# Layer 1's taps for the last sample: from one tap in 64x64 tiles to four taps at a time in 128x32 tiles

## The chip, the core and the metric

The kernel runs on one core of a Trainium2 chip. The core has five engines with instruction queues of their own: TensorE (PE, matrix products, with a separate row PEld for loading the stationary operand), VectorE (DVE), ScalarE (ACT), GpSimd (POOL) and SyncE (SP), which here only issues DMAs. The engines run side by side and wait for each other by semaphores; inside one engine the order is fixed. The metric is the device time of one launch in microseconds (us). Numbers are float32 throughout, and every matmul call of the program shows as two instruction records on PE.

## The reference, cut to what matters

The input is x of shape (4, 256, 48, 48): four samples, 256 channels (two halves k = 0, 1 of 128 channels), 2304 positions. Four layers are applied in turn, each as x = x + layer(groupnorm(x)): layer 0 is an attention of 8 heads, layer 1 a gate made by depthwise convolutions, layer 2 a second attention with one head, layer 3 a depthwise 3x3 convolution with normalisation. Layer 1, which the change touches, is:

```python
x_tem = _blur_pool(_max_pool_3x3(x), stride=3)            # 48x48 -> 16x16
x_h1 = _dwconv(x_tem, w_h1, ((5, 5), (1, 1)))             # 11x3 taps
x_w1 = _dwconv(x_tem, w_v1, ((1, 1), (5, 5)))             # 3x11 taps
x_h2 = _inv_h_transform(_dwconv(_h_transform(x_tem), w_h2, ((5, 5), (1, 1))))  # 11x3 along a diagonal
x_w2 = _inv_v_transform(_dwconv(_v_transform(x_tem), w_v2, ((1, 1), (5, 5))))
gate = sigmoid(batchnorm(x_h1 + x_w1 + x_h2 + x_w2))      # 16x16, then repeated 3x3
out = x * gate_upsampled
```

All four convolutions together are one depthwise convolution of a 16x16 image per channel with 81 distinct offsets (`TAPS`), whose weights are first gathered on a 13x13 grid per channel.

## The kernel before, in words

The order of all instructions is written out by the program itself. The main loop is `attend`. It goes through groups: a group is two blocks of 128 keys of one attention unit of 384 queries, and nine groups make a unit. In each group PE does the scores of this group (L309), then what is put in between (tables `fills` and `due`, and generators called lanes), then the weighted sum of the group before (L329). ScalarE takes the exponent (L315, `pt`), GpSimd adds the two blocks of a group (L340, `half`), VectorE adds these up (L355, `acc`). At the third group of the next unit the sums of the exponents are taken (`total`, L362), copied by ScalarE into two `row` tiles of the pool `op` (tag "o", two buffers), and sent through four small SP DMAs (L375); two groups later they are inverted (`invert`, L382 to L397) and spread by SP DMAs (L387, L392).

Layer 0 takes 864 groups, then layer 2 takes 27 groups for each of the four samples. We write group (s.g) for group g of 27 in the layer 2 attention of sample s. Other work rides in the groups: samples 0 to 2 have their layer 1 done during layer 0 of the sample behind them, on ScalarE and VectorE (`strips`). The last sample, b = 3, has its layer 1 done in the groups of layer 2 of samples 0 to 2, in the lanes of `l1_last`: `tops` (the maxima and the blur on VectorE, first k = 0 and then k = 1), `sums` (the 81 taps, on PE, `strips_pe`), and `gates` (the gate, the multiplication of x, the statistics for layer 2's norm). Each lane makes at most one step in a group, and none in groups 0, 9 and 18. `follow` waits for the norm's result `nb`, and two groups later starts the projections of sample 3 for its layer 2 (`start`, L1022 and L1028, and slices of L1058 and L1079). What is left of it in group (2.26) is emitted there at once, and sample 3's attention begins in (3.0).

`strips_pe` before: the blurred 16x16 image is put in the middle of a padded 28x28 tile `pd` (`padded`, memset by POOL at L856, filled by ACT at L859). A depthwise tap on PE is a product with a diagonal matrix of weights. `build` makes 12 such matrices of 64 columns on POOL (L927), `product` (L943) multiplies, with 64x64 tiles: the channels 0 to 63 and 64 to 127 apart, and the odd and the even taps apart, so that four tiles are in the array side by side. Rounds of 12 taps go to two PSUM tiles from `pj_tile` (a pool of two buffers that all the other work uses too), ScalarE copies them out in four pieces of 64x256 (L951), VectorE adds (L958, L961). There are seven rounds for each k, none of them in a group listed in `taken` (groups that already hold w_stats, a projection slice, or a `total`).

`w_stats` (L1112 on PE, L1120 on VectorE) also takes two `pj` tiles at a time and holds them until VectorE has read them. `gn` takes the group norm: `squares` (L228), `inverse` (L238, and the root on POOL, L179), `done` (L247 and L249 on VectorE, which give `nb`).

`tap_weights` prepares the tap weights once, in the first unit of layer 0: the grid, the list `wt` of 81 weights (L764), on POOL, one small piece in a group.

Of the kernel before, what the change touches and what calls it, by code (L numbers as in the profile page):

```python
# [14 lines left out]
P = 128  # L15
# [63 lines left out]
def usual_path(  # L79
# [648 lines left out]

    def tap_weights():
# [6 lines left out]
        nc.gpsimd.tensor_add(ident2, ident[:, 0:D], ident[:, D:P])  # L736
        yield 2
# [21 lines left out]
        while i < len(TAPS):  # L759
            dr, dc = TAPS[i]  # L760
            n = 1
            while i + n < len(TAPS) and TAPS[i + n] == (dr, dc + n):
                n += 1
            nc.gpsimd.tensor_copy(wt[:, :, i : i + n], g2[:, :, dr + 6, dc + 6 : dc + 6 + n])  # L764
            i += n
            yield 1
        v1 = lp.tile([P, NK], F32, name="v1")
# [6 lines left out]
    WEIGHT_TICKS = 26  # L774

    NT = 4
# [3 lines left out]
    L1_BUF = (NT + 1) * AS * AS  # L780
# [123 lines left out]
    TAPS_AT_ONCE = 12  # L904

    AT_PLACE = 7

    def strips_pe(b, k, norm, res):


        rounds = [
            range(i, min(i + TAPS_AT_ONCE, len(TAPS)))
            for i in range(0, len(TAPS), TAPS_AT_ONCE)
        ]
        diag = {}
        acc = lp.tile([P, AS, AS], F32, tag=("l1acc", "blur2")[k], name="l1acc")
        res["acc"] = acc
        parts = wo.rearrange("p c n -> p (c n)").rearrange(
            "p (i h r c) -> p i h r c", i=2, h=2, c=AS
        )  # L920

        def build(n):
            taps = rounds[n]
            xs = xsp.tile([P, NK, SL + 1], F32, tag="xs", name="diag1")
            xs = xs.rearrange("p k s -> p (k s)")[:, : len(taps) * D]
            diag[n] = xs.rearrange("p (t j) -> p t j", j=D)
            nc.gpsimd.tensor_tensor(  # L927
                diag[n], ident2.unsqueeze(1).to_broadcast([P, len(taps), D]),
                wt[:, k, taps[0] : taps[-1] + 1].unsqueeze(2).to_broadcast([P, len(taps), D]),
                ALU.mult,  # L930
            )

        def product(n):
            taps = rounds[n]
            ps = [pj_tile()[:, : AS * AS] for _ in HALVES]
            runs = [taps[0::2], taps[1::2]]
            for i in range(len(runs[0])):
                for h, r in enumerate(HALVES):
                    for e, run in enumerate(runs):
                        if i >= len(run):  # L940
                            continue
                        dr, dc = TAPS[run[i]]
                        nc.tensor.matmul(  # L943
                            ps[h][HALVES[h ^ e]].rearrange("p (r c) -> p r c", c=AS),
                            lhsT=diag[n][r, run[i] - taps[0], :],
                            rhs=pd[r, PAD + dr : PAD + dr + AS, PAD + dc : PAD + dc + AS],
                            start=i == 0, stop=i == len(run) - 1,
                        )
            for h, r in enumerate(HALVES):
                for e in range(2):  # L950
                    nc.scalar.copy(  # L951
                        parts[r, n % 2, e].rearrange("p r c -> p (r c)"), ps[h][HALVES[h ^ e]]
                    )

        def add(n):
            two = parts[:, n % 2]
            if n == 0:
                nc.vector.tensor_add(acc, two[:, 0], two[:, 1])  # L958
                return
            for e in range(2):  # L960
                nc.vector.tensor_add(acc, acc, two[:, e])  # L961
# [3 lines left out]
        while "blurred" not in res or "nb" not in norm:  # L965
            yield 1
        pd = padded(k, norm, res)
        res["padded"] = True
        yield 1
        for n in range(len(rounds)):  # L970
            while clock["t"] in taken:
# [1905 lines left out]
```

## Time and profile before

| what | value |
|---|---|
| median of 3 runs | 3520.81 us (3519.45 to 3521.15) |
| the profiled execution | 3522.7 us |
| its span, first to last instruction | 3520.9 us |
| granted TensorE clock, mean | 0.995 |
| layer 2 of samples 0, 1, 2, 3 begins at | 2904.1, 3020.7, 3155.5, 3266.1 us |
| the taps on PE (L943), first and last start | 2985.3, 3166.7 us |
| L943 records, busy | 648, 42.8 us |

A line of a group reads: line, engine, operation, tile written <- tiles read, array tile, shape, count | busy us, mean ns of one | idle time before it and what ended it. A line of a timeline reads: start, length, engine, line, operation, and in brackets the idle time before it and what ended it. Matmul records overlap, so the pace of PE is read from the distance of starts: 16 records of L309 start 1.29 us before the next 16 of L329.

### The profile page before, as it was taken

The numbers are of one execution on the slowest core, as the hardware profiler recorded it, in microseconds if no ns is written. First come the engines' busy times: TensorE is split into PE (matmuls) and PEld (weight loads), VectorE is DVE, ScalarE is ACT, GpSimd is POOL, SyncE is SP. The second block draws the span as 40 slices with busy tenths as digits, with TensorE's granted clock in tenths as the row PEclk, the third lists the DMA queues.
The fourth block names the chain that finished last, engine by engine and source line by source line (L and its number), as shares of the span: only waits on it lengthen the run. The fifth ranks groups of instructions, "written<-read, shape, count | busy, mean of one in ns | idle before, by whom it ended". The sixth has DMA issues, their size and how long they took to land. (4 is left out here: it accounts for less than half of the span.)

```text
span 3520.9 us, 88613 instructions
## 1 busy us (share of the span) xinstructions
PE 3438.4 (98%) x37158; PEld 1740.7 (49%) x37158; DVE 2559.1 (73%) x3456; ACT 2386.1 (68%) x3855; POOL 796.8 (23%) x666
## 2 busy tenths in 40 slices
PE   9999999999999999999999999999999999999988
PEld 5554555554444444444444444444444444555533
DVE  3555545467888788687887886878887878657777
ACT  5665666665886796557866976679668755555576
POOL 2333333321111000011110110101010106567432
PEclk9999999999999999999999999999999999999999
DMA  2211111111111111121111111111111110000067
GB/s 89 49 26 22 26 22 26 22 26 22 22 32 22 27 22 26 43 57 21 26 22 27 22 26 18 26 22 26 19 25 15 29 13 4 6 6 8 4 150 226
DMA packets 121897, 116.63 MB, mean 33 GB/s; under 512 B 58848, under 2 KB 112976, under 8 KB 120720
## 3 DMA queue, kind: packets, MB, share of 16 engines
q1 hardware_dynamic: 120240, 108.97, 16.4%
q8 instruction: 293, 4.80, 0.6%
q10 hardware_dynamic: 1248, 1.91, 0.2%
q14 instruction: 116, 0.95, 0.1%
HBM read 56.99 MB, written 11.80 MB: 20 GB/s over the span
## 5 line engine op out<-in xcount | busy, mean ns | idle before, releaser
L315 ACT ACTIVATE pt<-sc 128x768 f32<-128x768 f32 x1944 | 1474.8, 811 | 729.6 <-PE sc L309 722.0
L355 DVE TENSOR_TENSOR acc<-acc,pt 128x768 f32<-128x768 f32 x1368 | 1368.1, 1000 | 171.6 <-ACT pt L315 72.1
L329 PE MATMUL av<-pt,v 64*64 64x384 f32 x13824 | 1274.8, 484 | 0.0
L309 PE MATMUL sc<-q,k 64*64 64x384 f32 x13824 | 1270.0, 482 | 0.5 <-ACT pt L315 0.5
L309 PEld LDWEIGHTS sc<-q,k 64*64 64x64 f32 x13824 | 525.5, 133 | 589.4 <-issue 542.7
L329 PEld LDWEIGHTS av<-pt,v 64*64 64x64 f32 x13824 | 518.2, 133 | 599.1 <-issue 565.7
L410 POOL TENSOR_TENSOR o<-o,rinv 128x384 f32<-128x384 f32 x95 | 115.3, 1213 | 1731.2 <-DMA rinv<-rinv 1724.2
L340 POOL TENSOR_TENSOR half<-pt 128x768 f32<-128x768 f32 x189 | 363.0, 1924 | 532.2 <-ACT pt L315 492.5
L700 DVE SCALAR_TENSOR_TENSOR x<-pj,bo,x 128x384 f32<-128x384 f32 x192 | 118.5, 617 | 313.1 <-PE pj L687 311.7
L355 DVE TENSOR_TENSOR acc<-acc,half 128x768 f32<-128x768 f32 x171 | 192.2, 1124 | 207.4 <-POOL half L340 206.4
L876 ACT ACTIVATE prod<-pd,wt 128x256 f32<-128x256 f32 x486 | 337.3, 765 | 0.2
L604 PE MATMUL pj<-xs,w 128*128 128x384 f32 (+1 forms) x720 | 275.4, 505 | 0.0
L604 PEld LDWEIGHTS pj<-xs,w 128*128 128x128 f32 x720 | 124.1, 189 | 127.9 <-issue 38.3
L329 PE MATMUL av<-pt,qv 64*64 64x384 f32 x1728 | 174.7, 492 | 0.0
L309 PE MATMUL sc<-qv,kd 64*64 64x384 f32 x1728 | 171.6, 486 | 2.4 <-ACT pt L315 2.4
L899 DVE TENSOR_REDUCE prod<-prod 128x256 f32<-128x1280 f32 x114 | 168.7, 1480 | 0.7 <-ACT prod L876 0.7
L687 PE MATMUL pj<-o,wo 128*128 128x384 f32 (+1 forms) x384 | 160.1, 500 | 7.2 <-issue 3.6
L635 PEld LDWEIGHTS pj<-w,xs 128*128 128x128 f32 x1080 | 134.5, 191 | 24.2 <-issue 1.2
L349 DVE TENSOR_TENSOR acc<-pt 128x768 f32<-128x768 f32 x99 | 115.5, 1166 | 40.2 <-ACT pt L315 40.2
L406 POOL TENSOR_TENSOR o<-raw 128x384 f32<-128x384 f32 x95 | 128.9, 1357 | 50.5 <-ACT raw L402 50.0
L635 PE MATMUL pj<-w,xs 128*128 128x128 f32 x1080 | 134.9, 275 | 0.0
L402 ACT COPY raw<-av 128x768 f32<-128x768 f32 x108 | 86.3, 799 | 48.3 <-PE av L329 44.9
(291 smaller groups left out, 2421.2 us busy)
## 6 DMA issues: line engine op xcount, KB each, us to landing
xs<-in_x_dram SPq DMA_DIRECT2D x90, 384.0 KB
sh<-pad SPq DMA_DIRECT2D x126, 162.2 KB
rinv<-rinv SPq DMA_DIRECT2D x208, 94.5 KB
out_dram<-x SPq DMA_DIRECT2D x23, 384.0 KB
l<-row SPq DMA_DIRECT2D x416, 1.5 KB
w<-in_wqkv_dram SPq DMA_DIRECT2D x32, 192.0 KB
x<-in_x_dram SPq DMA_DIRECT2D x4, 1152.0 KB
x<-in_x_dram SPq DMA_DIRECT2D x9, 384.0 KB
```

Of the source, the lines that this page charges most:

```text
L309: nc.tensor.matmul(ps[c * D : (c + 1) * D, h, :SL], lhsT=u["of"]["k"][r, j0 : j0 + D], rhs=u["of"]["q"][r, u["qc"]], start=True, stop=True,)
L315: nc.scalar.activation(pt, ps[:, :, :SL], AF.Exp, scale=u["scale"])
L329: nc.tensor.matmul(u["av"][h * D : (h + 1) * D, half, :SL], lhsT=value(u, j, h)[r], rhs=pt[r, h, :], start=j == 0, stop=j == JB - 1,)
L340: nc.gpsimd.tensor_add(half, pts[0], pts[1])
L355: nc.vector.tensor_add(u["acc"], u["acc"], term)
L406: eng.tensor_add(u["sum"], u["raw"][:, 0, :], u["raw"][:, 1, :])
L604: nc.tensor.matmul(ps[:, :n], lhsT=at["w"][:, k, t, :], rhs=xs[s][:, k, :n], start=k == 0, stop=k == NK - 1,)
L635: nc.tensor.matmul(ps[:, i * P : (i + 1) * P], lhsT=xs[s][:, k, i * P : (i + 1) * P], rhs=at["w"][:, k, 2, :], start=k == 0, stop=k == NK - 1,
L687: nc.tensor.matmul(ps[:, :n], lhsT=wo[:, p, k * P : (k + 1) * P], rhs=o["o"][:, :n], start=True, stop=True,)
L700: nc.vector.scalar_tensor_tensor(xs, ps[:, :SL], pair["bo"][:, k : k + 1], xs, ALU.add, ALU.add)
L876: nc.scalar.activation(bufs[n % 3][:, :, min(n, 1) + i].rearrange("p (r c) -> p r c", c=AS), pd[:, PAD + dr : PAD + dr + AS, PAD + dc : PA ...
L899: nc.vector.tensor_reduce(to, bufs[n % 3][:, :, : min(n, 1) + len(taps)], AX.X, ALU.add)
```

## The change

The 81 offsets become sums over stacks. A stack is a set of four buffers, one for each block of 32 channels, whose four blocks of 32 partitions hold the same 32 channels of `pd`, shifted by 0, 1, 2 and 3 times a step. One matmul with 128 rows and 32 columns then applies four taps to 32 channels, and the four blocks j of 32 channels go to the four column tiles side by side. Four stacks per k (`STACKS`) with 9, 6, 3 and 3 products cover the taps: 21 products of 4 taps instead of 81 single ones. `place` fills a stack with 16 SP DMAs from SBUF to SBUF, each of 32 partitions with 465 to 634 float32; the buffers are tiles that are free at that time: the last attention output buffer `Y[1]` ("y"), `t1` and `t2` ("t", from the maxima), `t3` and `wo` ("w").

Both k go through one lane: eight stacks in the order `ORDER3`, ten rounds. Eight DMAs are issued in a step; a stack's product comes at the earliest three steps (`SETTLED`) after its last DMA was issued; a buffer set is filled again only after the products that read it have been emitted. A round now takes one PSUM tile, one ScalarE copy of 128x256 and, except for each k's first, one VectorE addition; the copy goes to a tile of tag "o" of the pool `op`. `gates` for a k starts when that k's last round was added.

`tap_weights` gets more work in the first unit of layer 0: 27 small POOL copies and a memset into `rolled`, a small POOL addition, and 16 SP DMAs of 32 partitions into `stacked`, the weights in the order in which the products read them.

```diff
@@ tap_weights
+        nc.gpsimd.tensor_add(ident2[:, 0:32], ident2[:, 0:32], ident2[:, 32:64])
...
+        rolled = lp.tile([P, L1_BUF], F32, tag="t3", name="rolled")
+        nc.gpsimd.memset(rolled[:, 0, :, 6:9], 0.0)
+        for q in range(4):
+            parts = [
...
+            for to, fr in parts:
+                nc.gpsimd.tensor_copy(to, fr)
+            yield 1
+        for q in range(4):
+            for j in range(4):
+                nc.sync.dma_start(
+                    stacked[32 * q : 32 * q + 32, j], rolled[32 * j : 32 * j + 32, q]
+                )
+            yield 1
...
-    WEIGHT_TICKS = 26
+    WEIGHT_TICKS = 34
...
+    STACKS = [
+        (PW + 5, PW, 634, [PW * a + c for a in (0, 4, 7) for c in range(3)]),
+        (5 * PW + 1, 1, 499, [PW * r + c for r in range(3) for c in (0, 7)]),
+        (8 * PW + 3, PW - 1, 465, [0, 1, PW + 1]),
+        (11, PW - 1, 465, [PW, PW + 1, 0]),
+    ]
+    ROUNDS3 = (((0, 6), (6, 9)), ((9, 15),), ((15, 18),), ((18, 21),))
+    ORDER3 = [
+        (0, 1, "y"), (0, 2, "y"), (0, 3, "y"), (0, 0, "t"), (1, 1, "w"), (1, 0, "t"), (1, 2, "w"),
+        (1, 3, "t"),
+    ]
+    FILLS_AT_ONCE = 8
+    SETTLED = 3
@@ strips_pe
         def build(n):
+            _, k, _, (m0, m1) = rounds[n]
...
+            shape = [P, m1 - m0, 4, 32]
             nc.gpsimd.tensor_tensor(
-                diag[n], ident2.unsqueeze(1).to_broadcast([P, len(taps), D]),
-                wt[:, k, taps[0] : taps[-1] + 1].unsqueeze(2).to_broadcast([P, len(taps), D]),
-                ALU.mult,
+                diag[n], ident2[:, 0:32].unsqueeze(1).unsqueeze(1).to_broadcast(shape),
+                stacked[:, :, k, m0:m1].rearrange("p j m -> p m j").unsqueeze(3)
+                .to_broadcast(shape), ALU.mult,
+            )
+        def place(u, n):
...
+            q, j = divmod(n, 4)
+            c0 = (j % 2) * size
+            nc.sync.dma_start(
+                bufs[u][j // 2][32 * q : 32 * q + 32, c0 : c0 + size],
+                pd[k][32 * j : 32 * j + 32, start + step * q : start + step * q + size],
             )
         def product(n):
-            ps = [pj_tile()[:, : AS * AS] for _ in HALVES]
...
+            ps = pj_tile()[:, : AS * AS]
+            for m in range(m0, m1):
+                for j in range(4):
+                    c0 = (j % 2) * size + offsets[m - FIRST3[i]]
+                    rhs = bufs[u][j // 2][:, c0 : c0 + AS * PW]
+                    nc.tensor.matmul(
+                        ps[32 * j : 32 * j + 32].rearrange("p (r c) -> p r c", c=AS),
+                        lhsT=diag[n][:, m - m0, j, :],
+                        rhs=rhs.rearrange("p (r c) -> p r c", c=PW)[:, :, 0:AS],
+                        start=m == m0, stop=m == m1 - 1,
                     )
-            for h, r in enumerate(HALVES):
-                for e in range(2):
-                    nc.scalar.copy(
-                        parts[r, n % 2, e].rearrange("p r c -> p (r c)"), ps[h][HALVES[h ^ e]]
+            if n == first[k]:
+                part[n] = None
+                nc.scalar.copy(acc[k], ps)
+            else:
+                part[n] = op.tile([P, SL + 1], F32, tag="o", name="part")[:, : AS * AS]
+                nc.scalar.copy(part[n], ps)
...
+        def may_fill(u, n):
+            k, _, which = ORDER3[u]
+            before = [v for v in range(u) if ORDER3[v][2] == which]
+            if before and n <= max(m for m, r in enumerate(rounds) if r[0] == before[-1]):
+                return False
+            if which != "y" and "blurred" not in res[1]:
+                return False
+            if k not in pd:
+                if "blurred" not in res[k] or "nb" not in norm:
+                    return False
+                pd[k] = padded(k, norm, res[k]).rearrange("p r c -> p (r c)")
+                res[k]["padded"] = True
+                return False
+            return True
 
         build(0)
         build(1)
+        left = [(u, c) for u in range(len(ORDER3)) for c in range(16)]
+        n, placed, seen = 0, {}, 0
+        while n < len(rounds):
+            add()
+            u = rounds[n][0]
+            if u in placed and seen >= placed[u] + SETTLED and clock["t"] not in taken:
+                product(n)
+                n += 1
+                if n + 1 < len(rounds):
+                    build(n + 1)
+            for _ in range(FILLS_AT_ONCE):
+                if not left or not may_fill(left[0][0], n):
+                    break
+                v, c = left.pop(0)
+                place(v, c)
+                if c == 15:
+                    placed[v] = seen
+            seen += 1
             yield 1
```

## The prediction

> **What bounds the kernel now.** I read the page's busy shares first, then the groups of PE in layer 2 (2904 to 3266 us), the busy times by stretch, the timeline of PE around the taps, and last the DMA issues of SP.
>
> ```profile
> PE 3438.4 (98%) x37158; PEld 1740.7 (49%) x37158; DVE 2559.1 (73%) x3456; ACT 2386.1 (68%) x3855; POOL 796.8 (23%) x666
> ```
>
> PE is the bound over the whole span. Whether it is so in the changed stretch is told by the stretches there (length; then busy PE, PEld, DVE, ACT, POOL; clock):
>
> ```profile
> 2985.00:3060.00 75.00, 67.99 (x832) 43.43 (x833) 59.24 (x69) 38.72 (x70) 46.60 (x25) 0.95 0.08 7
> 3060.00:3155.00 95.00, 88.70 (x1038) 56.11 (x1040) 47.20 (x62) 52.50 (x92) 57.94 (x33) 0.98 0.06 6
> 3155.00:3245.00 90.00, 84.34 (x1033) 49.57 (x1025) 72.47 (x88) 49.40 (x76) 70.30 (x38) 0.98 0.10 8
> ```
>
> PE is at 91 to 94%, so it leads, but VectorE is at 79% and 81% in the first and third stretch, and the clock dips below 1. The groups say how much of PE is taps, and that 128x32-like tiles already run in layer 3 (96*32):
>
> ```profile
> L943 PE MATMUL pj<-pd,diag 64*64 64x256 f32 x648 | 42.8, 399 | 9.8 <-DVE bst L1120 6.7 <-ACT pd L859 3.1
> ```
>
> ```profile
> L309 PE MATMUL sc<-q,k 64*64 64x384 f32 x13824 | 1270.0, 482 | 0.5 <-ACT pt L315 0.5
> ...
> L1730 PE MATMUL cv<-sh,taps 96*32 96x384 f32 (+1 forms) x1152 | 104.5, 503 | 1.8 <-DMA sh<-pad 1.1 <-ACT junk L1593 0.7
> ```
>
> Busy time over records is 91.9 ns for L309 and 90.7 ns for L1730: a record of 32-column tiles costs what a record of 64x64 tiles costs, four being in the array at once in both. The timeline gives the pace and the stalls:
>
> ```profile
> 2931.18 1.47 PE L309 MATMUL sc<-qv,kd 64*64 64x384 f32 x16
> 2932.58 2.85 PE L1058 MATMUL pj<-x,w 128*128 128x384 f32 x8
> ...
> 2985.32 2.93 PE L943 MATMUL pj<-pd,diag 64*64 64x256 f32 x48 [3.06 <-ACT pd L859]
> ...
> 3016.76 2.88 PE L943 MATMUL pj<-pd,diag 64*64 64x256 f32 x48
> 3019.41 1.52 PE L329 MATMUL av<-pt,qv 64*64 64x384 f32 x16
> ...
> 3050.89 5.44 PE L943 MATMUL pj<-pd,diag 64*64 64x256 f32 x48 [4.07 <-DVE bst L1120]
> ...
> 3085.18 1.63 PE L309 MATMUL sc<-qv,kd 64*64 64x384 f32 x16 [2.41 <-ACT pt L315]
> ...
> 3205.63 1.37 PE L1112 MATMUL pj<-y,Ww 64*64 64x384 f32 x5 [4.08 <-DVE bst L1120]
> ```
>
> An undisturbed round of 48 records takes 3019.41 - 3016.76 = 2.65 us of PE, 55.2 ns a record. Around the rounds PE stands still where VectorE is late with `bst`, and where ScalarE waits for `pd`.
>
> **PE's stream: -17.2 us.** Before: 81 taps x 2 halves of channels x 2 k = 324 calls, 648 records, x 55.2 ns = 35.8 us. After: 21 products x 4 blocks x 2 k = 168 calls, 336 records of the same 256 columns, 18.6 us.
>
> **Switching the array's tiles: +2.2 us.** The old rounds were 64x64 between 64x64 neighbours; the new ones switch to 128x32 and back, 10 rounds x 2. The row: L309's 16 records cost 1.29 us, yet L1058, in 128*128, starts 1.40 us after them, so a switch costs 0.11 us and 20 cost 2.2. The Trainium skill ("TensorEngine Tiling (Array Packing)", Tiling Modes, Key Properties) speaks against the change: a change of tiling mode drains the array. It gives no time; if a drain costs the constant of an isolated matmul, 398 cycles at 2.4 GHz = 0.166 us ("TensorE: Matmul & The Clock Gate", Single matmul latency), 20 make 3.3 us as an estimate and the sum is 1.1 us worse. I take the row.
>
> **ScalarE, VectorE and POOL per round: nothing by themselves.**
>
> ```profile
> L927 POOL TENSOR_TENSOR diag<-ident,wt 128x768 f32<-128x768 f32 (+1 forms) x14 | 29.1, 2082 | 31.8 <-PE pj L943 31.8
> L951 ACT COPY wo<-pj 64x256 f32<-64x256 f32 x56 | 20.5, 366 | 33.6 <-PE pj L943 32.7
> L961 DVE TENSOR_TENSOR l1acc<-l1acc,wo 128x256 f32<-128x256 f32 x24 | 16.3, 677 | 11.1 <-ACT wo L951 9.9
> ```
>
> ScalarE goes from 56 to 10 copies (20.5 to about 4 us; the copy of twice the partitions has the same 256 columns), VectorE from 26 additions to 8 (18.7 to 5.4 us), POOL from 10368 to 5376 elements in `build` (29.1 to 15 us). ScalarE's gain hides behind PE; VectorE's shows only through its stalls, next.
>
> **Stalls of PE that were there.** (a) 3.06 us for `pd` at group (0.20): POOL's memset only ended at 2984.6 and ScalarE, held by `pd`, can't take the next exponent either. With the round gone, PE meets the same wait at the scores of (0.21) instead. -0.4. (b) 4.07 us at (1.6), and the round then took 5.44 us instead of 2.65: 6.9 us in all. In (0.20) to (1.6) PE loses 13.3 us of old rounds (five, 2.65 each) against 4 us of new ones; VectorE loses 6.3 us of additions (L958, L961) and some of POOL's interference. PE comes some 11 us earlier, VectorE, which waited 6.2 us for POOL at 3023 when POOL stood behind a `build` that waited for a round, comes perhaps 10 earlier. Between 0 and -6.9; I take half, -3.5. (c) 2.41 us at (1.13) for the second `pd`, when two builds of 3.6 us stood before the memset on POOL; they no longer do. But the memset now waits until 16 fills have read the old `pd`. Between 0 and -4, I take -2. (d) 4.08 us at (2.14): the gate's work on VectorE moves, see below; 0, between -2 and +3.
>
> The clock: after 4.07 us of standing the 48 records took 2.8 us too long, after 3.06 us nothing was lost (2.93). The skill ("TensorE: Matmul & The Clock Gate", Part 1) says that an idle window of about 3.4 us halves the clock, in agreement; by it any new wait over that length costs about 2 us more, by the rows of this trace waits up to 3 us cost only themselves. My new waits stay below.
>
> **The fills: +2.5 us.**
>
> ```profile
> L1607 SPq DMA_DIRECT2D sh<-pad x126: 507/588/1824, 3364.4 to 3486.4; - x126
> ```
>
> ```profile
> 2992.22 2.43 SPq L375 DMA_DIRECT2D l<-row  x4
> ```
>
> 128 fills at 0.588 us are 75 us of SP, 9.4 us a stack, and SP is otherwise almost empty here (10 issues a unit). What they move, 8.4 MB (16 x 32 rows x 634, 499, 465, 465 float32, twice), is light: layer 3 moved 202 GB/s. By the code's rules the steps come out so: `pd` in (0.19), fills (0.20, 0.21), rounds at (0.24), (1.2), (1.6), (1.15), (1.19), (1.20), (1.24), (1.26), (2.1), (2.6). The same counting reproduces where the old rounds stand in the trace. At (0.24): eight fills run from 2985.3 to 2990, the four `l` DMAs of (0.21) come next and end near 2992.5, the other eight end near 2997 and have landed by 2999, while PE gets there near 2997: 2 us of waiting. At (1.6) the margin is about zero, elsewhere three groups or more remain. Queued behind the fills are `l` and `rinv`; in (1.19) to (1.23) SP falls 10 us behind, but `rinv` of that unit is wanted only four groups and a projection slice later (about 20 us). Between 0 and +8.
>
> **Two "o" buffers: +1.5 us.** Round (1.2) writes a `part`, its addition is emitted in (1.3) behind `total`, whose second `row` needs the same buffer. So ScalarE's row copy waits until VectorE is through the maxima of that step (L831, L832: 3.7 us in the trace), with the next exponent behind it. Between 0 and +4.
>
> **The end of the chain: +3 us, and +1.** The last old round is at (2.2), the gate at (2.4), `nb` at (2.23), `start` at (2.25). The new last round is at (2.6), the gate at (2.7), `squares` at (2.22), `inverse` at (2.24), `nb` and `start` both at (2.26), the last group. There PE waits: the root on POOL comes after VectorE's L240, so `half` of (2.24), which ended at 3242.3, ends near 3244.9, its `acc` near 3246, `nb` near 3247, and PE would be there at 3243.9. 3 us, between 0 and 7. `squares` and `inverse` also need `pj` tiles next to w_stats in (2.22): +1.
>
> **Weights in layer 0: 0.** 27 copies (17 such took 5.4 us), and 16 DMAs (9.4 us), in a stage where POOL is busy 13 to 20 us of 40 and waits for ScalarE. Without that cover some 9 us of POOL would show.
>
> **Sum:** -17.2 + 2.2 - 0.4 - 3.5 - 2 + 2.5 + 1.5 + 3 + 1 = -12.9 us. The profiled execution of 3522.7 us (1.8 us of it outside the span) becomes 3509.8. The median lies 1.9 us under that execution, so 3507.9 us.
>
> **Rivals.** *VectorE sets the pace* in the first and third stretch: stalls (b) and (c) keep their length (+5.5 against my sum), the additions of (1.3) cost 4 (+2.5), and the late gate crowds VectorE at (2.11) to (2.14) where w_stats waits for it (+2): -2.9, 3518 us. For it: 79 to 81% and the `bst` waits. Against it: 52 us of VectorE's idle time in layer 2 are waits for POOL, which gets lighter. *The stalls go wholly*: (b) -6.9, (c) -4, no wait for fills: -20.8, 3500 us. *Late fills, slower than before*: each product waits for its stack in PE's order, and nothing passes it. It decides from 12.9 / 8 = 1.6 us per stack beyond my sum. At 3 us per stack, +24, the kernel takes 3532 us. For it: only three short groups (7.7 us) between the last eight issues and the product, 4.7 us of issuing and the `l` DMAs between. Against it: most groups here last 3 to 6 us, and in layer 3 the first product after 16 such issues waited 1.07 us for a DMA. *That the tiles don't run four abreast* would leave a stream of 18.6 us longer; L1730 excludes it.
>
> **How the numbers follow.** My case 0.61, with a range of its own of 3503 to 3513; stalls gone 0.13; VectorE's pace 0.18; late fills 0.08. A measurement here can tell 0.2%, 7 us, from no change: above 3513.8 is "same". Faster: 0.93 of my case, all of the second, a fifth of VectorE's, 0.74 or about 0.75; slower is the last case, 0.08, and 0.17 is left for the same. The range of 8 in 10 leaves out the slow case and the best tail: 3499 to 3518.5.
>
> **What would show it.** Right: 336 records for the taps in about 21 us busy; the rounds in the groups named; the round at (1.6) without a dip of the clock; `start` in the last group of sample 2's attention behind a wait for `nb`; layer 3 and layer 0 unchanged in length. Wrong: PE's idle time before the taps released by a DMA for more than 13 us in all; or layer 2 of sample 1 as long as before in spite of fewer records, with `bst` as the releaser.

## The result, and the profile after

| | before | after |
|---|---|---|
| median (8 runs each, side by side) | 3520.97 us (3517.73 to 3523.21) | 3508.83 us (3505.00 to 3512.72) |
| ratio, with its 95% interval | 1 | 0.9965 (0.9956 to 0.9974) |
| the profiled execution; its span | 3522.7; 3520.9 us | 3510.3; 3508.6 us |
| tap records on PE, busy | 648, 42.8 us | 336, 24.8 us |

The changed kernel is 12.1 us faster; 3507.9 us was predicted. The share of busy time hardly moves, since PE leads in both:

```profile
PE 3430.5 (98%) x36846; PEld 1721.6 (49%) x36846; DVE 2543.4 (72%) x3438; ACT 2369.3 (68%) x3809; POOL 798.9 (23%) x691
```

The groups of layer 2 (line, engine, tile, shape, count | busy, mean ns | idle before, releaser) show the three kinds of buffers of the taps, and the lighter work of GpSimd, ScalarE and VectorE:

```profile
L1016 PE MATMUL pj<-stack,diag 128*32 128x256 f32 x204 | 16.8, 422 | 2.1 <-issue 2.1
...
L971 POOL TENSOR_TENSOR diag<-ident,stacked 128x384 f32<-128x384 f32 (+1 forms) x10 | 14.3, 1438 | 28.6 <-PE pj L1016 28.6
...
L1016 PE MATMUL pj<-y,diag 128*32 128x256 f32 x96 | 8.0, 437 | 4.0 <-DVE bst L1216 4.0
...
L1033 DVE TENSOR_TENSOR l1acc<-l1acc,part 128x256 f32<-128x256 f32 x8 | 6.6, 826 | 7.4 <-ACT part L1027 7.4
...
L1016 PE MATMUL pj<-wo,diag 128*32 128x256 f32 x36 | 4.4, 387 | 0.0
...
L1027 ACT COPY part<-pj 128x256 f32<-128x256 f32 x8 | 3.0, 372 | 15.2 <-PE pj L1016 10.8 <-issue 4.4
```

No idle time of PE ahead of L1016 is put down to a DMA. What PE waited for in layer 2 (us in total, times, longest):

```profile
PE pj L1016 <- DVE bst L1216: 4.0, 2, 2.1
PE pj L1208 <- DVE bst L1216: 3.6, 2, 3.5
...
PE pj L1208 <- ACT row L371: 2.5, 1, 2.5
```

The taps waited 6.7 us for `bst` and 3.1 us for `pd` before; now 4.0 us for `bst`, 2.1 us for "issue" (which the last experiment resolves), and `w_stats` waits in other places. An undisturbed round of 24 records, and three of the places where PE stands, look so on PE's timeline:

```profile
3102.89 1.47 PE L309 MATMUL sc<-qv,kd 64*64 64x384 f32 x16
3104.29 1.53 PE L1016 MATMUL pj<-stack,diag 128*32 128x256 f32 x24
3105.75 1.52 PE L329 MATMUL av<-pt,qv 64*64 64x384 f32 x16
3107.09 1.47 PE L309 MATMUL sc<-qv,kd 64*64 64x384 f32 x16
...
3193.16 2.01 PE L1208 MATMUL pj<-y,Ww 64*64 64x384 f32 x8 [3.49 <-DVE bst L1216]
...
3221.38 0.38 PE L228 MATMUL pj<-mx,gmat 128*128 128x2 f32 x2 [2.43 <-DVE bst L1216]
...
3236.18 0.61 PE L1118 MATMUL pj<-gn_nb,w2c 128*128 128x1 f32 x4 [1.13 <-DVE gn_nb L249]
```

From 3102.89 to 3104.29 are 1.40 us where L309's 16 records cost 1.29; the 24 records take 1.46 us where 24 x 55.2 ns are 1.32; the next 16 take 1.34 us instead of 1.29. So a round pays 0.11 + 0.14 + 0.05 = 0.30 us for its change of tiles.

Each unit of attention has one sum of exponents (L362 in groups (s.3), (s.12), (s.21)), which marks the same place in every kernel. The changed kernel was profiled three times in all (here, and twice below). From one L362 to the next, with the prediction's sum cut up at the same places (tap records x 55.2 ns, 0.22 us a round for tiles, and its other terms where it put them):

| from, to | before | after, three profiles | mean difference | predicted |
|---|---|---|---|---|
| (0.12), (0.21) | 37.9 | 35.0, 34.8, 34.6 | -3.1 | -3.1 |
| (0.21), (1.12) | 89.9 | 84.4, 83.0, 83.5 | -6.3 | -8.8 |
| (1.12), (1.21) | 46.7 | 40.0, 41.7, 41.7 | -5.6 | -2.7 |
| (1.21), (2.3) | 41.8 | 42.3, 40.7, 40.7 | -0.6 | -4.0 |
| (2.3), (2.12) | 25.8 | 26.8, 26.8, 26.8 | +1.0 | +1.5 |
| (2.12), (2.21) | 32.1 | 31.7, 31.7, 29.2 | -1.2 | 0 |
| (2.21), (3.3) | 48.1 | 52.4, 52.5, 54.5 | +5.0 | +4 |
| sum | 322.4 | 312.7, 311.1, 310.9 | -10.9 | -12.9 |

Before was profiled once, in an execution 1.7 us above its median; the three of the changed kernel lie 3.3 us below theirs in the mean. So a row is good to one or two us.

Outside these units no term was predicted. There the recorded execution of after lost 1.6 us between the first score of layer 2 and the first L362, and from the last one to the end took 241.4 us for 245.8 (241.1 and 240.4 in its other two profiles). Of these 4.8 us in the mean, 1.5 come from the change: up to the first L1601 of layer 3 all three profiles took 82.4 or 82.5 us, and before took 83.9 to the same place, with one more wait of 1.05 us for `bst`; the run that moves the last stack, below, brings both back. Most of the rest differs between executions: the kernel before with light rounds, below, took 242.3 us for the whole stretch.

### The profile page after: what moved, and what is told of

Same layout as the page of the kernel before. It is cut to its first block, busy times and chain, and to the rows that moved or that the text cites. A ratio compares the mean times of both kernels' runs of the same rounds, so it can differ in the third digit from the quotient of the medians.

```text
span 3508.6 us, 88105 instructions
## 1 busy us (share of the span) xinstructions
PE 3430.5 (98%) x36846; PEld 1721.6 (49%) x36846; DVE 2543.4 (72%) x3438; ACT 2369.3 (68%) x3809; POOL 798.9 (23%) x691
## 5 line engine op out<-in xcount | busy, mean ns | idle before, releaser
L355 DVE TENSOR_TENSOR acc<-acc,pt 128x768 f32<-128x768 f32 x1368 | 1369.1, 1001 | 173.6 <-ACT pt L315 74.6
L309 PE MATMUL sc<-q,k 64*64 64x384 f32 x13824 | 1270.2, 483 | 0.5 <-ACT pt L315 0.5
L309 PEld LDWEIGHTS sc<-q,k 64*64 64x64 f32 x13824 | 526.1, 133 | 588.8 <-issue 542.1
L700 DVE SCALAR_TENSOR_TENSOR x<-pj,bo,x 128x384 f32<-128x384 f32 x192 | 118.5, 617 | 312.3 <-PE pj L687 310.9
L355 DVE TENSOR_TENSOR acc<-acc,half 128x768 f32<-128x768 f32 x171 | 186.5, 1090 | 207.7 <-POOL half L340 207.0
L309 PE MATMUL sc<-qv,kd 64*64 64x384 f32 x1728 | 168.6, 492 | 1.2 <-ACT pt L315 1.1
L406 POOL TENSOR_TENSOR o<-raw 128x384 f32<-128x384 f32 x95 | 128.7, 1355 | 48.4 <-ACT raw L402 48.1
```

The lines of the kernel that those rows point to most:

```text
L309: nc.tensor.matmul(ps[c * D : (c + 1) * D, h, :SL], lhsT=u["of"]["k"][r, j0 : j0 + D], rhs=u["of"]["q"][r, u["qc"]], start=True, stop=True,)
L355: nc.vector.tensor_add(u["acc"], u["acc"], term)
L406: eng.tensor_add(u["sum"], u["raw"][:, 0, :], u["raw"][:, 1, :])
```

## The experiments

Theory: the gain is PE's shorter stream of taps, less a few waits that the new order makes. Rivals: the gain is the lighter work of the helpers; the fills limit it; VectorE has become the bound. Line numbers of the experiments are up to five higher than the changed kernel's; those of the light rounds go with the kernel before (L944 there for L943, L1108 for L1112, `bst` L1116 for L1120).

**Twice and a third of the products.** Dose for PE's stream, the helpers' work unchanged.

```diff
-                    nc.tensor.matmul(
+                    for twice in range(2):
+                        nc.tensor.matmul(
...
-                        start=m == m0, stop=m == m1 - 1,
+                            start=m == m0 and twice == 0, stop=m == m1 - 1 and twice == 1,
```

> The changed kernel with each of the 168 calls for the taps issued twice, so the sum of the taps comes out doubled; all else is as it was: the same fills, copies, additions and builds. PE's stream of taps is 672 records instead of 336, close to the 648 of the kernel before, but without its 46 extra copies and 18 extra additions. Theory (the gain is PE's stream): 336 records at 55 ns put back 18.5 us, so 3508.8 + 18.5 = about 3527 us, between 3522 and 3531, a little above the kernel before. Rival (the gain came from the lighter rounds of ScalarE, VectorE and GpSimd, and PE's records mostly fell into its waits): less than 8 us come back, below 3517 us.

```diff
+            m1 = m0 + (m1 - m0) // 3
             for m in range(m0, m1):
```

> The changed kernel with only the first third of each round's products: 112 records for the taps instead of 336, all copies, additions, builds and fills as they were (54 of the 81 taps, padded weights of zero aside, are left out of the sum). In the run with doubled products 336 more records made the stretch from the first sum of the exponents to (2.21) 15.2 us longer, 45 ns a record, and the time 16 us. Theory (PE's stream sets the pace on the way down too): 224 records fewer give 10 us, between 8 and 12.5 us below the changed kernel. Rival (with the changed kernel VectorE has become the bound of layer 2, at 79 to 81% busy and with most of PE's waits put down to bst): less than 4 us.

Doubled: 3523.45 us, 1.0012 of before (1.0006 to 1.0019). A third: 3491.17 us, 0.9923 (0.9911 to 0.9936). The L362 of (0.12) and of (2.21) on PE's timeline, first of the changed kernel, then doubled, then a third:

```profile
2954.47 0.82 PE L362 MATMUL pj<-acc,ones 64*64 64x384 f32 x8
...
3214.75 0.97 PE L362 MATMUL pj<-acc,ones 64*64 64x384 f32 x8
```

```profile
2952.25 0.82 PE L362 MATMUL pj<-acc,ones 64*64 64x384 f32 x8
...
3226.08 0.97 PE L362 MATMUL pj<-acc,ones 64*64 64x384 f32 x8
```

```profile
2949.42 0.82 PE L362 MATMUL pj<-acc,ones 64*64 64x384 f32 x8
...
3194.16 0.97 PE L362 MATMUL pj<-acc,ones 64*64 64x384 f32 x8
```

That is 260.3, 273.8 and 244.7 us; the mean of the three profiles of the changed kernel is 258.5. 336 records more cost 15.4 us there (46 ns each), 224 fewer give 13.7 us (61 ns each), around the 55 ns of the prediction; the three profiles of the changed kernel themselves lie between 256.4 and 260.3 us. Single rounds are free of that scatter. The round of 24 records above has 8 in the run with a third:

```profile
3092.55 0.65 PE L1017 MATMUL pj<-stack,diag 128*32 128x256 f32 x8
3093.13 1.52 PE L329 MATMUL av<-pt,qv 64*64 64x384 f32 x16
```

0.58 us for 1.46: 16 records are 0.88 us, 55 ns each. In the medians the gain of the third is 20 us against the changed kernel beside it; the expectation of 8 to 12.5 us was too small. Of the 6 us that these units do not show, 2 lie in the first stretch of layer 2 (46.9 us for a mean of 49.1, by the clock, see below), and most of the rest is that the profiled executions of the changed kernel were faster than its median: their mean is 3507.0 us, 17.5 above that of the third. The rival "VectorE is now the bound" would have given under 4 us: it falls. The theory's main term stands in both directions.

**The kernel before with light rounds.** One copy, one VectorE operation and half a build per round, PE's 648 records kept.

```diff
-                diag[n], ident2.unsqueeze(1).to_broadcast([P, len(taps), D]),
+                diag[n], ident2.unsqueeze(1).to_broadcast([P, half, D]),
...
-            for h, r in enumerate(HALVES):
-                for e in range(2):
-                    nc.scalar.copy(
-                        parts[r, n % 2, e].rearrange("p r c -> p (r c)"), ps[h][HALVES[h ^ e]]
-                    )
+            nc.scalar.copy(parts[:, n % 2, 0].rearrange("p r c -> p (r c)"), ps[1])
...
-            for e in range(2):
-                nc.vector.tensor_add(acc, acc, two[:, e])
+            nc.vector.tensor_add(acc, acc, two[:, 0])
```

> The kernel before with all 648 tap records on PE, but with its other engines' work per round cut to about that of the changed kernel: one copy of 128x256 on ScalarE instead of four of 64x256, one VectorE operation instead of two, builds of 6 matrices instead of 12. It leaves out the products of one PSUM tile in each round and reads wrong weights for half of the taps. Theory: PE's stream is what counts, and of the lighter rounds only stalls (b) and (c) of the prediction, 5.5 us, can go: between 0 and 5.5 us below the kernel before, 3515.5 to 3521 us. Rival (lighter rounds): most of the 12 us of the change, so 3509 to 3513 us.

Measured: 3516.92 us, 0.9990 of before (0.9982 to 0.9998), some 2 to 4 us (1 to 6 by the interval). PE's waits in layer 2:

```profile
PE pj L944 <- DVE bst L1116: 5.0, 3, 2.1
...
PE pj L1108 <- DVE bst L1116: 4.1, 1, 4.1
PE pj L944 <- ACT pd L859: 3.1, 1, 3.1
```

The taps' wait for `bst` at (1.6) goes from 4.07 to 1.81 us, while the one at (1.15) grows from 1.56 to 2.09; the other two lines keep their length. So lighter helpers alone give a quarter or so of the change, by the interval at most about half; the rival falls, and stall (b) is shown to depend on them in part. The gain stands in the medians alone: from (0.12) to (3.3) the profiled execution took 324.0 us for 322.4, with dips of the clock (0.57 from 3146 to 3152 us).

**The fills: each one twice, then each one in two halves.**

```diff
+            for _ in range(2):
                 nc.sync.dma_start(
```

> The changed kernel with every one of the 128 fill DMAs issued twice in a row, to the same place: 75 us more of SP, 9.4 us a stack, counted in the same groups. In the trace of the changed kernel no wait of PE is put down to a DMA, but the first stack's last fill landed at 3001.1 us and its product started at 3002.05 us, 1 us later. Theory (fills are hidden, with little margin at the first stack and three groups or more at the others): about 8 us at the first stack less what its wait for bst (1.9 us) covers, up to 3 us at the third one, nothing elsewhere: +6 to +11 us, 3515 to 3520 us. Rival (the fills and their queue are what the change pays with, in every stack): +3 us or more for each of eight stacks, above 3532 us. Second rival (there is slack everywhere): below 3511 us.

Measured: 3732.61 us, 1.0608 of before (1.0593 to 1.0622). Neither expectation foresaw 214 us, and the edit did more than double the issues: the second DMA writes where the first has just written and waits for it to land. SP's waits from 2900 to 3300 us:

```profile
SPq L1004 <- DMA stack<-pd: 70.2, 44, 4.3
SPq L1004 <- DMA y<-pd: 68.6, 48, 4.0
```

It measured an ordering of DMAs that the change doesn't have. So the next one cut each fill in two, with the same bytes and no place written twice:

```diff
-            nc.sync.dma_start(
-                bufs[u][j // 2][32 * q : 32 * q + 32, c0 : c0 + size],
...
+            cut = size // 2
+            for a, z in ((0, cut), (cut, size)):
+                nc.sync.dma_start(
+                    bufs[u][j // 2][32 * q : 32 * q + 32, c0 + a : c0 + z],
```

> The changed kernel with each fill cut into two DMAs of half the columns: 256 DMAs, the same bytes, 9.4 us more of SP per stack, and no DMA writes where another has written. From SP's timeline of the changed kernel the stacks' last issues stand before their products by: 1 us (first), 10 us (second), 1 us (third), 17, 16, 8, 11 and 9 us. Theory (an issue of 0.6 us is what a fill costs, and the fills are hidden only by these distances): the first product comes 8 us later, the second 2, the third 9, the sixth and eighth 1 each, less 4 us of bst waits that fall into them: +14 to +22 us, 3520 to 3530 us. Rival (the fills have slack everywhere, what the run with doubled fills lost came only from a DMA waiting for the one before it): less than 5 us, below 3512 us.

Measured: 3555.27 us, 1.0098 of before (1.0083 to 1.0113), 44.5 us above the changed kernel beside it: more than twice the theory's upper end. From its waits of PE, then its timelines of PE, SP and VectorE:

```profile
PE pj L1018 <- DMA y<-pd: 17.7, 12, 8.4
```

```profile
3205.81 1.82 PE L1018 MATMUL pj<-stack,diag 128*32 128x256 f32 x12 [4.11 <-DVE bst L1218]
```

```profile
3176.61 24.07 SPq L1005 DMA_DIRECT2D stack<-pd  x32
```

```profile
3195.42 1.62 DVE L355 TENSOR_TENSOR acc<-acc,half 128x768 f32<-128x768 f32 x1
3204.77 0.17 DVE L382 TENSOR_TENSOR ls<-l 128x6 f32<-128x6 f32 x1 [7.73 <-DMA l<-row]
...
3205.19 1.02 DVE L1218 BATCH_NORM_STATS2 bst<-pj 128x6 f32<-128x384 f32 x2
```

The products' own waits are 17.7 us where 19 were expected of the first three stacks (8.4 us at the first, as worked out). Of the rest the trace shows two ways. At (2.6) 32 fills stood ahead of the `l` DMAs on SP until 3200.8 us, VectorE stood 7.7 us for `l` in `invert`, the `bst` behind it was late, and PE's next work waited for its PSUM tile; the unit from (2.3) to (2.12) took 40.3 us for 26.8, at a mean granted clock of 0.83. At (1.13) GpSimd's memset for the second `pd` waited for fills that still read the first, ScalarE for the memset, and PE's scores for ScalarE:

```profile
POOL pd L886 <- DMA stack<-pd: 4.9, 1, 4.9
...
ACT pd L889 <- POOL pd L886: 7.3, 1, 7.3
```

```profile
3094.84 2.84 PE L309 MATMUL sc<-qv,kd 64*64 64x384 f32 x16 [5.08 <-ACT pt L315]
```

So the fills are hidden in the changed kernel, but only just: twice as many issues cost nearly four times what the change gains.

**The parts in a buffer of their own.**

```diff
+                if n in (1, 2):
+                    part[n] = wo.rearrange("p c n -> p (c n)")[:, : AS * AS]
+                else:
+                    part[n] = op.tile([P, SL + 1], F32, tag="o", name="part")[:, : AS * AS]
```

> The changed kernel with the copies of its second and third rounds (groups (1.2) and (1.6)) put in the tile wo, which is free then, instead of a tile of tag o; the order of all instructions stays. Theory (two o buffers): the row copy of (1.3), which waited 6.29 us for VectorE's addition and held PE back by 2.47 us, no longer waits, and nothing takes its place: 2 to 4 us below the changed kernel, 3505 to 3507 us. Rival: the wait only moves to the next bst wait, VectorE being late either way: within 1 us of the changed kernel.

Measured: 3502.29 us, 0.9956 of before (0.9942 to 0.9970), an interval that holds the changed kernel's 0.9965. ScalarE and PE of the changed kernel, then of this one:

```profile
3038.78 0.48 ACT L371 COPY row<-pj 128x384 f32<-128x384 f32 x1 [6.29 <-DVE l1acc L1033]
```

```profile
3026.50 0.87 ACT L371 COPY row<-pj 128x384 f32<-128x384 f32 x2
```

```profile
3036.21 1.01 PE L1211 MATMUL pj<-y,Ww 64*64 64x384 f32 x5 [2.26 <-DVE bst L1219]
```

The copy no longer waits, but PE, which had lost 2.47 us to it, loses 2.26 us to `bst` close behind. VectorE is late there in part because its L355 at 3033.12 us ran beside GpSimd's `half` and took 2.56 us; in the changed kernel, ahead of the same `bst`, it took 0.95. Over (0.21) to (1.12) the four profiles with this edit took 83.3, 83.5, 80.1 and 81.4 us, those without it (three of the changed kernel, one with the next edit) 84.4, 83.0, 83.5 and 83.5: 1.5 us in the mean, less than the first four differ among themselves. By the traces the rival was the nearer one; the medians, with overlapping intervals, can't tell the two.

**The changed kernel twice more.**

> The changed kernel as it is, as the base for the three others, and to see which of its profile's differences come back. Theory (in layer 2 before the first round, and in layer 3, the instructions are those of before, and their differences of +3.3 and -4.4 us came from how the clock was granted in one execution): the first stretch, from the first score to the first sum of the exponents, takes 46.5 to 47.5 us as in the other four kernels, not 50.2 us; from there to layer 3 the execution repeats the recorded one within 2 us; the median is 0.9965 of the kernel before. Rival (the change itself slows the first stretch, by the tiles or DMAs it adds): 50 us again.

> The changed kernel once more, as the base of the three others: 0.9965 to 0.9969 of the kernel before. In its profile the stretch from the sum of (0.12) to that of (2.21) should be 258 to 261 us and from there to (3.3) 52.4 us, as in the two profiles of it so far; before had 274.3 and 48.1.

Measured: 3510.79 us, 0.9969 (0.9960 to 0.9979), and 3511.26 us, 0.9977 (0.9969 to 0.9986): 11.1 and 7.8 us below before. The units repeat as the table shows, within 2.6 us; of the second one's 258 to 261 and 52.4 us, 256.4 and 54.5 came. The first stretch of layer 2, in which no instruction was changed, as rows by stretch (length; then PE, PEld, VectorE, ScalarE and GpSimd busy; clock): the changed kernel, its second profile, and the kernel with the parts in `wo`:

```profile
2904.00:2954.50 50.50, 48.22 (x472) 23.11 (x468) 38.68 (x52) 24.92 (x38) 28.94 (x17) 0.93 0.02 3
```

```profile
2904.00:2952.70 48.70, 46.42 (x468) 22.57 (x462) 40.50 (x47) 24.77 (x38) 29.31 (x17) 0.96 0.02 3
```

```profile
2902.00:2949.00 47.00, 44.72 (x468) 21.98 (x464) 40.49 (x47) 24.77 (x38) 29.30 (x17) 1.00 0.02 3
```

50.2, 48.6 and 46.9 us from the first score to L362, in steps of about 1.7 us, each with its clock. Neither expectation was exact. The kernel before took 48.6 us too, and 46.9 with light rounds; it is the granted clock and not the change.

**The last stack in Y[1].**

```diff
-        (1, 3, "t"),
+        (1, 3, "y"),
```

> The changed kernel with one word of ORDER3 changed: the last stack goes to the buffer Y[1] instead of t1 and t2, which it would have to wait for. By the counting of steps only the last round moves, from (2.6) to (2.2), and with it the second gate, the statistics and the end of the chain by four groups. Theory (the late end of the chain costs what the prediction said: waits for nb and at squares): the 1.13 us wait for nb at (2.26) and the 2.43 us wait at (2.22) with its slow clock go, 2 to 5 us below the changed kernel, 3502 to 3505 us. Rival (VectorE is late there whatever comes when: the gate's work only meets other w_stats): within 1.5 us of the changed kernel.

Measured: 3506.38 us, 0.9961 of before (0.9948 to 0.9975), 4.4 us below the changed kernel beside it, with intervals that overlap. The stretch from L362 of (2.21) to that of (3.3), of the changed kernel and of this one:

```profile
3214.70:3267.20 52.50, 46.16 (x433) 28.19 (x429) 20.36 (x27) 28.33 (x48) 23.25 (x14) 0.97 0.05 5
```

```profile
3208.40:3256.50 48.10, 43.83 (x426) 25.83 (x422) 18.04 (x25) 28.00 (x48) 21.40 (x13) 1.00 0.06 5
```

48.1 us is what the kernel before takes, and all four profiles with this edit have it; the waits for `nb` and at `squares` (L228) are gone, and with them the dip of the clock. So the late end of the chain costs 4.3 us in this stretch. Of these some 1.5 us come back: up to L1601 of layer 3 this kernel then takes 84.0 us for 82.4, as before did (83.9), with one more wait of 1.05 us for `bst`.

**Both edits, and the gate in two steps.**

> Both edits in one: parts of the second and third rounds in wo, last stack in Y[1]. In the profile of the first of them alone the row copy no longer waited, but PE then waited 2.26 us for bst in the same place, and the two units there took 1.0 us less, not 2 to 4. Theory (they are apart, one in sample 1, one in sample 2): their gains add up, 3 to 6 us below the changed kernel. Rival (VectorE is the limit in both places): 0 to 2 us below it.

> Parts in wo and last stack in Y[1], once more beside the changed kernel, for an interval. Theory: the last stack takes 4.3 us from the stretch between (2.21) and (3.3), as in its two profiles (48.1 for 52.4 us), and the parts at most 1.5 us: 4 to 6 us below the changed kernel, a ratio of 0.995. Rival: its first median, 6.7 us below, or the one trace, 3.4 us, was chance, and it is within 2 us of the changed kernel.

```diff
         nc.vector.reciprocal(gate, gate)
+        if split:
+            yield 1
         nc.vector.tensor_scalar(acc, gate, norm["nb"][:, k : k + 1], None, ALU.mult)
```

> The kernel with both edits (parts in wo, last stack in Y[1]) and one more: the gate of k = 0 makes its four VectorE operations (L1088 to L1091 of the changed kernel) in two steps, so two of them, 1.41 and 0.35 us long, come behind the bst of (1.24) instead of ahead of it; PE's order is the same. Theory (PE's stand of 2.05 us ahead of the round of (1.24), which the profile puts down to issue, is VectorE's bst behind the gate): 1.5 to 2 us of that stand go, and the clock no longer halves there; the unit from (1.21) to (2.3) gets 1.5 to 3.5 us shorter, the kernel 1.5 to 3.5 us faster than with the two edits alone. Rival (something else, such as the queue of instructions, makes the stand): it stays at 2.05 us.

| | time | of before | the changed kernel beside it |
|---|---|---|---|
| both edits | 3504.08 | 0.9949 (0.9936 to 0.9963) | 0.9969 (0.9960 to 0.9979) |
| both edits, again | 3504.31 | 0.9958 (0.9945 to 0.9971) | 0.9977 (0.9969 to 0.9986) |
| and the gate in two steps | 3504.66 | 0.9952 (0.9940 to 0.9965) | 0.9977 (0.9969 to 0.9986) |

Both edits give about 0.2% twice, 7 us. From (0.12) to (3.3) their profiles took 307.7 and 303.7 us, 3.9 and 7.9 less than the mean of the changed kernel; behind it they took 2.5 us more (243.6 and 243.5 for a mean of 241.0), so the traces show less than the medians. With the split gate the interval lies wholly below the changed kernel's, but it can't be told from the two edits alone. PE's stand ahead of the round of (1.24) went from 2.05 to 1.47 us, a third of what was expected; whether the clock profits can't be told, since the round behind took 3.13 us and 3.12 and 3.14 in two of the three profiles without the edit. VectorE in the changed kernel's second profile, then VectorE and GpSimd with the split gate:

```profile
3120.48 1.41 DVE L1090 TENSOR_SCALAR l1acc<-gate,gn_nb 128x256 f32<-128x256 f32 x1
3121.92 0.35 DVE L1091 TENSOR_SCALAR gate<-gate,gn_rs 128x256 f32<-128x256 f32 x1
3122.19 0.95 DVE L355 TENSOR_TENSOR acc<-acc,half 128x768 f32<-128x768 f32 x1
...
3123.47 1.02 DVE L1216 BATCH_NORM_STATS2 bst<-pj 128x6 f32<-128x384 f32 x2
```

```profile
3121.82 2.19 DVE L355 TENSOR_TENSOR acc<-acc,half 128x768 f32<-128x768 f32 x1
...
3124.34 1.02 DVE L1221 BATCH_NORM_STATS2 bst<-pj 128x6 f32<-128x384 f32 x2
3125.28 0.34 DVE L1095 TENSOR_SCALAR l1acc<-gate,gn_nb 128x256 f32<-128x256 f32 x1
```

```profile
3121.39 1.81 POOL L340 TENSOR_TENSOR half<-pt 128x768 f32<-128x768 f32 x1 [1.42 <-ACT pt L315]
```

PE's scores before the round began at 3120.60 and 3122.07, so `bst` comes 2.87 and then 2.27 us after them: 0.60 us sooner, and the stand is 0.58 us shorter. It follows `bst`, as the theory said. The 1.76 us that were moved gave so little because L355, which now runs beside GpSimd's `half`, took 2.19 us instead of 0.95. Before the edit it was L1090 that ran beside `half`, for 1.41 us; in its new place the same operation (L1095) takes 0.34. In both kernels the operation of VectorE that met `half` was the long one, and the edit chose another.

## Why the prediction was right, and where it was not

The time came out 0.9 us above the forecast, and the ten rounds stand in exactly the ten groups named, but in the units -10.9 us came where -12.9 were worked out, and terms of 2 to 3 us were wrong in both directions. The main term was right; that the sum came so near is in part luck, since the errors cancel, and since the same comparison gave 12.1, 11.1 and 7.8 us on its three occasions.

- **PE's stream, -17.2 us: right.** 336 records are there; the dose runs give 46 and 61 ns a record around the 55.2 used, and 55 in an undisturbed round.
- **Switching, +2.2 us: too small.** The rule that was weighed and put aside (the Trainium skill, "TensorEngine Tiling (Array Packing)", Key Properties: a change of mode drains the array) was nearer: 0.30 to 0.32 us a round in the undisturbed rounds make 3.1 us for ten, where the estimate by the rule was 3.3; that it is a drain no run shows. The row that was used showed only one side of a switch; the round itself and the next 16 records pay too.
- **Helpers, 0 by themselves: right**, shown by the run with light rounds.
- **Stall (a), -0.4: right in kind.** The `pd` wait moved to the scores of (0.21): 1.1 us in the first profile, 2.4 and 2.3 in the others, for 3.1, so -0.7 to -2.
- **Stall (b), -3.5, fills, +2.5, and "o" buffers, +1.5.** In (0.21) to (1.12) these were to add +0.5 and came as about +2.7 by the table (-6.3 against -9.0 of stream and switching, the latter at 0.31 us a round). The fills cost nothing: the first product waited 1.88 us, but for `bst`. The buffers cost PE 2.47 us, and without them VectorE would have cost most of that. Stall (b) did shrink from 4.07 to 2.12 us (1.25 and 1.32 in the other profiles), but what PE saved it spent on those waits. It was also counted 0.4 us too high: 5.44 us is the old round's length with the end of its last record, and to the next start it took 5.07. The step that failed here is "PE comes some 11 us earlier, VectorE perhaps 10": the round of (1.6), released by VectorE's `bst` before and after, started 98.2 us after the L362 of (0.12) before and 93.6, 92.1 and 92.3 after, so VectorE came 4.6 to 6.2 us earlier. That part of the rival "VectorE sets the pace" was right.
- **Stall (c), -2: too small.** The unit lost 5.6 us, of which stream and switching explain 0.4. The 2.41 us wait, a slow clock behind it that the prediction did not see (1.7 us, see the last item), and a wait of 1.56 us for `bst` at the round of (1.15) all went, the last not for good.
- **The gate of k = 0 against `w_stats` at (1.24): missing from the sum.** The prediction looked for this collision only at (2.14) and after the second gate. The first gate, too, now stands between two `bst`: 2.05 us in each of the three profiles, and the round behind it 0.3 to 2 us longer. That is the 3 us by which (1.21) to (2.3) fell short. Before, the same gate (L992 to L995, from 3089.17 us) stood between two `bst` at (1.15), and PE waited 1.56 us for the second of them: the wait moved with the gate from one unit to the next.
- **(d), 0: right.** The stand at (2.14) is 3.49 us for 4.08. From (2.12) to (2.21) VectorE was busy 31.69 of 32.1 us before and 30.21 of 31.7 after, so PE's stream could not shorten that unit.
- **The chain's end, +3 and +1: right in sum, not in parts.** `nb` cost 1.13 us; at `squares` it was 2.43 us and a slow clock. From (2.12) to (3.3) the three profiles took 84.1, 84.2 and 83.7 us, before 80.2, and the kernel with the last stack in Y[1] 80.3: the end cost 3.4 to 3.9 us there, and gave 1.5 back in front of layer 3's L1601.
- **Weights in layer 0, 0: right.** Layer 2 began at 2904.28 us for 2904.11.
- **"Waits up to 3 us cost only themselves": wrong.** The trace of before already spoke against it. Behind the 2.41 us at (1.13) its clock was 0.53, 0.50 and 0.59 in three stretches from 3086.5 to 3090.2 us, and 16 records took 2.35 us from start to start instead of 1.29:

```profile
3087.85 2.58 PE L329 MATMUL av<-pt,qv 64*64 64x384 f32 x16
3090.20 1.52 PE L309 MATMUL sc<-qv,kd 64*64 64x384 f32 x16
```

The rival "late fills" did not happen, but the split fills show its price: its mechanism has two more paths, one that the prediction named and dismissed, the `l` DMAs behind the fills and VectorE behind `l`, and one that it named under stall (c) alone, the second `pd` behind the fills that read the first. "The stalls go wholly" failed at (0.21) to (1.12).

## What to carry to other kernels

When the bound engine's stream shrinks, count what is saved there in full, and then look in every unit for the engine that is second: here the same `bst` waits came back a group or two later, and two of three patches to single waits gave a fraction of the wait, because an operation of VectorE then ran beside GpSimd's and took 1.2 and 1.6 us longer. Work that is moved must be laid beside everything that waits in its new place, each copy of it; one gate was checked for that and the other not. A queue that hides its issues can still be at its edge, so work out, for each transfer behind them, when it would land if the issues doubled.

## What the hardware showed

- **The clock after short stands.** Two stretches of the changed kernel's round at (1.24), behind a stand of 2.05 us, in its first profile (clock 0.50) and, later in the round, in its second (1.00):

```profile
3127.50:3129.50 2.00, 2.00 (x25) 1.88 (x19) 2.00 (x3) 0.00 (x0) 0.00 (x0) 0.50 0.32 79
```

```profile
3125.60:3127.30 1.70, 1.70 (x34) 1.24 (x24) 1.70 (x3) 0.00 (x0) 0.00 (x0) 1.00 0.29 69
```

The same 48 records took 4.79 us in the one and 3.12 in the other; undisturbed they take 2.81. Behind a stand of 1.88 us at (0.24) they took 3.26 us, and 5.36 with both edits. The Trainium skill ("TensorE: Matmul & The Clock Gate", Part 1) puts the idle window at about 3.4 us; these stands are shorter, and the clock halved in some executions and not in others, so the measurement decides against it as a lower limit. (The page also says that the window runs freely, so the same kernel meets it in different phases. That would fit the difference between executions, though not a stand shorter than the window; no run here shows the window itself.) The two rounds differ by 1.67 us, and a single profile can't tell such a step from a change.
- **Two ends of a tile switch**: 0.11 us ahead of a round, 0.14 to 0.17 in it, 0.05 in the 16 records behind it.
- **VectorE beside GpSimd**: L355 on the same shapes took 0.95 us with GpSimd idle and 1.74 to 2.56 us at other times, so moving VectorE's work by two us can change its length by one. The 2.19 us with the split gate ended 0.81 us after `half`, the 2.56 us with the parts in `wo` 0.82 us after it. The skill ("SBUF — State Buffer", two separate sides) says that a VectorE instruction with two SBUF inputs and a GpSimd one that reads SBUF lock a shared port pair against each other for the whole instruction; both, begun with `half` running, agree in kind.
